# Handing out other work between the four tiles of an image's first attention chunk

## The chip, the core and the metric

The kernel runs on one core of a Trainium2 chip. The metric is the device time of one launch in microseconds (us). The time before is the median of three runs. The profile is one further execution, with the profiler on.

## What is computed

Two images of 128 channels and 64 x 64 pixels pass two layers, all in 32-bit floats. Layer 0 is a group norm and a windowed attention (7 x 7 neighbours, 4 heads) with norms and linear maps around it. Layer 1 takes the 4096 pixels of each image as tokens. It has two parts, and the change lies in the first of them:

```python
# layer 0
x = x + conv_attn(group_norm(x))
# layer 1, first part: attention of an image's 4096 tokens over themselves
t = to_tokens(x)
q = layernorm(t)
sim = (q @ q.T) * 128 ** -0.5
sim[diagonal] = -1e9
t = t + softmax(sim) @ q
# layer 1, second part: long convolution with 16 filters, done in the frequency domain,
# and three short lags, with weights picked by log_w + gumbel
t = t + spectral(layernorm(t)) + short_lags(layernorm(t))
out = from_tokens(t)
```

The attention of layer 1 runs over all 4096 tokens of one image: `sim` is 4096 x 4096 for each image and is symmetric, since queries and keys are the same array.

## The kernel before

**Engines and stages.** Below, PE is TensorE, DVE is VectorE, ACT is ScalarE, POOL is GpSimd, and SP is the engine that issues most transfers. In time the kernel has three stages. Layer 0 of both images takes the first 345 us of the profiled execution. Layer 1's attention runs first for image 0 (from 345.8 us), then for image 1 (from 812.7 us). The convolution in the frequency domain starts at 1295.6 us and lasts to the end.

**The attention, `attention(b, fill)`, line 882.** The 32 tiles of 128 tokens of an image are grouped into 8 chunks of 4 tiles. Because `sim` is symmetric only the 36 pairs of chunks `(a, c)` with `c >= a` are computed. `weights(a, c, k)` makes one tile: a matmul over 128 channels into a PSUM bank (L903[...]), for a diagonal pair an addition that masks the diagonal (DVE, L909), the exponential with its row sums (ACT, L911), and for a diagonal pair the part left of the diagonal, which is turned from the tiles made earlier by transposes on PE (L917) and copied by DVE (L918). So in a diagonal pair tile `k` needs the finished exponentials of tiles 0 to `k-1`. `turned` makes the transposed tiles of a pair off the diagonal (PE L927, DVE L930). `onto` adds a tile's product with the tokens to the chunk `a` itself (L941, PSUM tile `own`), and L968 adds those for chunk `c` (PSUM tile `other`).

**The order.** The four tiles of the first pair (0, 0) are made ahead of the loop, one behind the other. In the loop over pairs, each of the four steps of a pair makes one tile of the *following* pair, multiplies one tile of the present pair onto its chunk, and then calls `fill()`.

**`fill()`, lines 1207 to 1229.** It hands out one step of other work: it takes the generator at the head of a list and runs it to its next `yield`. First comes `urgent`, what follows an image's finished chunks; then `steps`, a list given by the caller. A `yield True` ends the turn of that list and gives out nothing more from it. The instructions of a step are written into the program at that place. The order in which they reach an engine's queue is mostly that of the program, but not always: the framework's own ordering puts forward instructions that it expects to be ready. In this stage no order by hand is in force (the `manual_schedule` blocks at L844 and L1379 cover layer 0 and the convolution).

**What image 0's attention hands out.** `steps` begins with `drain()` (L1231): the rest of layer 0, 72 pieces, three to a step. The first four steps are:

| step | pieces | work |
|---|---|---|
| 1 | k.a, k.tt, k.bn | four transposes of `xa` (PE L200), a copy to `tt` (ACT L684), statistics (DVE L691, L693): the last four token tiles of image 0 |
| 2 | t.yr, k.pw, k.z | POOL alone: a maximum (L660), the reciprocal root of those four tiles (L698, L699), their normalised values `tok` (L704) |
| 3 | t.proj, t.pb, t.add | eight matmuls (PE L602), DVE L613, POOL L636 and L638 |
| 4 | t3.bn, k.b, k.cm | DVE L379 and L381, four transposes of the new `tok` (PE L193), a copy to `cm` (ACT L716) |

Behind the drain come `branch_weights` (L1081), `filters` (L1154) and image 1's `tokens` (L204).

**What image 1's attention hands out.** `steps` begins with what image 0 has left over: the remaining steps of `after` for its chunks 6 and 7, then `short_lags`. `after(b, c, part)` (L985) has seven: (1) transposes of `xa` (PE L992) and the weighted sum into `tt` (DVE L997); (2) a layer norm to `z` (DVE L174, L175, L164; POOL L165; DVE L182); (3) nothing, a `yield True`; its next turn transposes `z` (PE L193) and copies it to `zc` (ACT L1009); (4) and (5) four matmuls each (PE L1028), copies to `ub` by ACT and DVE (L1030) and two stores each (SP L1017); (6) eight small matmuls (PE L1038), copies (L1044) and four stores (SP L1046). Behind these come `filter_matrices` (L1137), whose loads go through SP (L1130) and whose mixing runs on DVE (L1133, L1135, L1146 to L1151), and `load_blocks` (SP L1270).

Of the kernel before, what the change touches and what calls it, by code (L numbers as in the profile page):

```python
# [95 lines left out]
def kernel(  # L96
# [761 lines left out]
    with ap_:  # L858
# [6 lines left out]
        def bank():  # L865
            return ps_m.tile([P, 512], F32, tag="bank", name="bank")
# [15 lines left out]
        def attention(b, fill):  # L882
# [15 lines left out]
            def weights(a, c, k, left=()):  # L898

                n = 4 * CHUNKS[a] + k  # L900
                lo = k * P if a == c else 0
                ps = bank()
                nc.tensor.matmul(  # L903
                    ps[:, lo:], lhsT=cm[b][:, n * P : (n + 1) * P],
                    rhs=cm[b][:, CHUNKS[c] * 512 + lo : (CHUNKS[c] + 1) * 512], start=True, stop=True,
                )
                if a == c:
                    ks = slice(k * P, (k + 1) * P)
                    nc.vector.tensor_tensor(ps[:, ks], ps[:, ks], ndiag, ALU.add)  # L909
                e = ep.tile([P, 512], F32, tag="e", name="e")  # L910
                nc.scalar.activation(  # L911
                    e[:, lo:], ps[:, lo:], AF.Exp, bias=0.0, scale=ASCALE, accum_out=part[:, n, c : c + 1]
                )
                if lo:
                    pt = bank()
                    for j in range(k):
                        nc.tensor.transpose(pt[:, j * P : (j + 1) * P], left[j][:, lo : lo + P], ident)  # L917
                    nc.vector.tensor_tensor_reduce(  # L918
                        e[:, 0:lo], pt[:, 0:lo], one[:, 0:lo], 1.0, 0.0, ALU.mult, ALU.add, part[:, n, 8:9]
                    )  # L920
                return e

            def turned(a, c, m, es):

                pt = bank()
                for k in range(4):
                    nc.tensor.transpose(pt[:, k * P : (k + 1) * P], es[k][:, m * P : (m + 1) * P], ident)  # L927
                et = ep.tile([P, 512], F32, tag="et", name="et", bufs=4)
                n = 4 * CHUNKS[c] + m
                nc.vector.tensor_tensor_reduce(  # L930
                    et, pt, one, 1.0, 0.0, ALU.mult, ALU.add, part[:, n, a : a + 1]
                )
                return et
# [3 lines left out]
            def onto(a, n, e, first, last):  # L937
                nonlocal own
                if first:
                    own = ps_o.tile([P, 512], F32, tag="own", name="own")  # L940
                nc.tensor.matmul(own, lhsT=tok[b][:, n, :], rhs=e, start=first, stop=last)  # L941
                if last:
                    xs = xa[b][:, chunk(a)]
                    if a:
                        nc.vector.tensor_tensor(xs, own, xs, ALU.add)
                    else:
                        nc.vector.tensor_copy(xs, own)
                    fill(CHUNKS[a], part)
# [2 lines left out]
            es = []  # L951
            for k in range(4):
                es.append(weights(0, 0, k, es))
            for i, (a, c) in enumerate(pairs):
                following = pairs[i + 1] if i + 1 < len(pairs) else None
                coming = []
                if a != c:
                    other = ps_o.tile([P, 512], F32, tag="other", name="other")
                for k in range(0, 4, 2):
                    for j in (k, k + 1):  # L960
                        if following:
                            coming.append(weights(*following, j, coming))
                        if a == c:
                            while late:
                                onto(*late.pop(0))
                            onto(a, 4 * CHUNKS[a] + j, es[j], j == 0, a == 7 and j == 3)
                        else:
                            nc.tensor.matmul(  # L968
                                other, lhsT=tok[b][:, 4 * CHUNKS[a] + j, :], rhs=es[j], start=(j == 0), stop=(j == 3)
                            )  # L970
                        if late:
                            onto(*late.pop(0))
                        fill()
                    if a != c:
                        for j in (k, k + 1):
                            late.append((a, 4 * CHUNKS[c] + j, turned(a, c, j, es), False, c == 7 and j == 3))
                if a != c:
                    xs = xa[b][:, chunk(c)]
                    if a:
                        nc.vector.tensor_tensor(xs, other, xs, ALU.add)  # L980
                    else:
                        nc.vector.tensor_copy(xs, other)
                es = coming
# [223 lines left out]
        def filler(b, steps, kept=None):  # L1207

            urgent, done = [], []

            def fill(c=None, part=None):
                if c is not None:
                    done.append(c)
                    urgent.append(after(b, c, part))
                    if len(done) % 4 == 0:
                        held = kept if kept is not None and len(done) == 4 else urgent
                        held.append(short_lags(b, len(done) // 4 - 1))
                    return

                for queue in (urgent, steps):  # L1220
                    while queue:
                        got = next(queue[0], False)
                        if got is None:
                            return
                        if got:
                            break
                        queue.pop(0)

            return fill, urgent
# [17 lines left out]
        steps = [drain(), chosen, filters(), tokens(1, bank)]  # L1247
        fill, left = filler(0, steps)
        attention(0, fill)
        for gen in steps:  # L1250
            for _ in gen:
# [30 lines left out]
        kept = []  # L1282
        fill, left = filler(1, steps, kept)
        attention(1, fill)
        for gen in steps:
            for _ in gen:
# [237 lines left out]
```

## Time and profile before

| | |
|---|---|
| time, median of 3 runs | 2200.89 us (2199.68 to 2202.2) |
| the profiled execution's own time | 2200.82 us |
| its span, first to last instruction | 2199.1 us |
| outside the span | 1.7 us |
| PE busy | 2145.5 us, 98% of the span |
| DVE busy | 952.8 us, 43% |
| ACT busy | 769.9 us, 35% |
| POOL busy | 278.7 us, 13% |
| mean granted TensorE clock | 0.992 |

All times of single instructions below are microseconds from the span's start in this one execution. A profile line of an instruction group reads: start, length, engine, line, operation, output and inputs, count, and in brackets how long the engine had been idle and what released it. The modelled ends of matmuls overlap the next ones, so the cost of a matmul in a stream is read from one start to the next.

### The profile page before, as it was taken

How to read it: one execution, taken by the hardware profiler on the slowest of the kernel's cores; microseconds unless marked ns; L12 is line 12 of the kernel's file. 1: busy time of each engine (PE TensorE's matmuls, PEld its weight loads, DVE VectorE, ACT ScalarE, POOL GpSimd, SP SyncE). 2: the span in 40 equal slices, each digit the busy share in tenths (PEclk: the TensorE clock that was granted, in tenths of full speed). 3: DMA queues.
4: the chain of work that ended last, by engine and by line, in shares of the span. 5: the costliest groups of instructions: out<-in, count | busy, mean ns of one | idle time of the engine just before them, and what ended most of it. 6: DMA issues, size and time to landing. Idle time of an engine off the chain costs nothing.

```text
span 2199.1 us, 32064 instructions
## 1 busy us (share of the span) xinstructions
PE 2145.5 (98%) x12016; PEld 1341.3 (61%) x12016; DVE 952.8 (43%) x3150; ACT 769.9 (35%) x1904; POOL 278.7 (13%) x357
## 2 busy tenths in 40 slices
PE   6999998999999999999999999999999999999998
PEld 4677774545555444544554456767767676767776
DVE  5899985444443356433333543232232323232232
ACT  3889884222332222122223233232232323232232
POOL 3477875200000000000000000000000000000000
PEclk8999999999999999999999999999999999999999
DMA  4222212021000025000001142221221221212101
GB/s 147 62 61 61 62 52 53 0 74 47 25 24 25 23 67 159 24 24 25 1 24 31 44 109 50 50 60 40 60 52 48 50 50 44 56 44 56 40 11 77
DMA packets 170347, 110.56 MB, mean 50 GB/s; under 512 B 21311, under 2 KB 155087, under 8 KB 169680
## 3 DMA queue, kind: packets, MB, share of 16 engines
q1 hardware_dynamic: 169266, 105.01, 17.8%
q8 instruction: 95, 1.56, 0.3%
q0 software_dynamic: 576, 2.10, 0.3%
q10 hardware_dynamic: 350, 1.41, 0.3%
q14 instruction: 60, 0.49, 0.1%
HBM read 73.86 MB, written 34.63 MB: 49 GB/s over the span
## 4 chain that ended last, share of the span: by engine, by line
PE 89%; DVE 5%; POOL 3%; ACT 1%; DMA 1%; issue 1%; SPq 0%; POOLq 0%; DVEq 0%; ACTq 0%
PE acc L1348 25%; PE pc L1336 13%; PE own L941 11%; PE bank L903 10%; PE other L968 8%; PE bank L927 4%; PE bank L333 2%; PE bank L1069 2%; PE bank L543 2%; PE bank L193 2%; PE bank L1028 1%; PE py L1370 1%; PE bank L507 1%; PE po L565 1%; ACT p L530 1%; POOL ln_rs L387 1%
## 5 line engine op out<-in xcount | busy, mean ns | idle before, releaser
L1337 DVE COPY y<-pc 128x512 f32<-128x512 f32 x320 | 221.5, 692 | 351.7 <-PE pc L1336 348.0
L911 ACT ACTIVATE e<-bank 128x512 f32<-128x512 f32 (+3 forms) x288 | 161.6, 561 | 513.9 <-PE bank L903 396.7
L1348 PE MATMUL acc<-y,mpl 128*128 128x256 f32 x1280 | 292.1, 382 | 0.0
L1348 PE MATMUL acc<-y,mmi 128*128 128x256 f32 x1280 | 288.0, 379 | 0.0
L1336 PE MATMUL pc<-ct,ut 64*128 64x512 f32 x1280 | 285.2, 595 | 1.0 <-issue 1.0
L903 PE MATMUL bank<-cm 128*128 128x512 f32 (+3 forms) x576 | 278.4, 565 | 1.4 <-DVE y L654 1.4
L1348 PEld LDWEIGHTS acc<-y,mpl 128*128 128x128 f32 x1280 | 238.1, 190 | 59.4 <-issue 29.6
L1348 PEld LDWEIGHTS acc<-y,mmi 128*128 128x128 f32 x1280 | 242.6, 190 | 32.6
L1337 ACT COPY y<-pc 128x512 f32<-128x512 f32 x320 | 204.5, 639 | 87.0 <-PE pc L1336 86.9
L941 PE MATMUL own<-et,tok 128*128 128x512 f32 x448 | 228.6, 597 | 6.5 <-DVE part L930 6.4
L968 PE MATMUL other<-e,tok 128*128 128x512 f32 x448 | 229.9, 595 | 0.0
L1336 PEld LDWEIGHTS pc<-ct,ut 64*128 64x128 f32 x1280 | 121.5, 187 | 145.9 <-issue 140.7
L930 DVE CUSTOM_DVE_ANT_0 et<-bank,one 128x512 f32<-128x512 f32 x224 | 145.4, 686 | 131.3 <-PE bank L927 131.3
L941 PEld LDWEIGHTS own<-et,tok 128*128 128x128 f32 x448 | 84.4, 191 | 116.9 <-issue 67.1
L1355 ACT COPY ob<-acc 128x256 f32<-128x256 f32 x32 | 19.3, 604 | 387.1 <-PE acc L1348 387.1
L1372 DVE TENSOR_TENSOR xa<-py,xa 128x512 f32<-128x512 f32 x32 | 22.1, 691 | 281.4 <-PE py L1370 281.4
L968 PEld LDWEIGHTS other<-e,tok 128*128 128x128 f32 x448 | 81.9, 191 | 90.1 <-issue 88.5
L927 PEld LDWEIGHTS bank<-ident,e 128*128 128x128 f32 x896 | 102.9, 141 | 55.4 <-issue 50.2
L903 PEld LDWEIGHTS bank<-cm 128*128 128x128 f32 x576 | 94.2, 191 | 65.1 <-issue 41.6
L165 POOL TENSOR_TENSOR ln_rs<-ln_rs,mhalf 128x4 f32<-128x4 f32 x24 | 24.5, 1019 | 811.2 <-DVE ln_rs L164 811.2
L530 ACT ACTIVATE p<-p,mn 128x196 f32<-128x196 f32 x256 | 114.3, 449 | 14.0 <-DVE mn L520 13.5
L927 PE MATMUL bank<-ident,e 128*128 128x128 f32 x896 | 117.2, 274 | 0.0
(215 smaller groups left out, 2342.5 us busy)
## 6 DMA issues: line engine op xcount, KB each, us to landing
ut<-us SPq DMA_DIRECT2D x80, 256.0 KB
us<-ub SPq DMA_DIRECT2D x64, 256.0 KB
vw<-vd SPq DMA_DIRECT2D x256, 49.0 KB
ct<-gs SPq DMA_DIRECT2D x160, 72.0 KB
ct<-gs SPq DMA_DIRECT2D x160, 64.0 KB
gs<-sum SPq DMA_DIRECT2D x20, 256.0 KB
vd<-v SPq DMA_DIRECT2D x128, 32.0 KB
st<-in_m_plus_dram SPq DMA_DIRECT2D x16, 256.0 KB
```

Source lines behind the costliest of these rows:

```text
L193: nc.tensor.transpose(ps[:, j * P : (j + 1) * P], src[:, j, :], ident)
L333: nc.tensor.matmul(pl, lhsT=wg[:, lo : lo + P], rhs=zT, start=True, stop=True)
L530: nc.scalar.activation(p, p, AF.Exp, bias=t[name + "mn"][:, h : h + 1], scale=-1.0, accum_out=t["den"][:, u, h : h + 1],)
L903: nc.tensor.matmul(ps[:, lo:], lhsT=cm[b][:, n * P : (n + 1) * P], rhs=cm[b][:, CHUNKS[c] * 512 + lo : (CHUNKS[c] + 1) * 512], start=True, ...
L911: nc.scalar.activation(e[:, lo:], ps[:, lo:], AF.Exp, bias=0.0, scale=ASCALE, accum_out=part[:, n, c : c + 1])
L927: nc.tensor.transpose(pt[:, k * P : (k + 1) * P], es[k][:, m * P : (m + 1) * P], ident)
L930: nc.vector.tensor_tensor_reduce(et, pt, one, 1.0, 0.0, ALU.mult, ALU.add, part[:, n, a : a + 1])
L941: nc.tensor.matmul(own, lhsT=tok[b][:, n, :], rhs=e, start=first, stop=last)
L968: nc.tensor.matmul(other, lhsT=tok[b][:, 4 * CHUNKS[a] + j, :], rhs=es[j], start=(j == 0), stop=(j == 3))
L1336: nc.tensor.matmul(pc, lhsT=ut[fp, b, par, :], rhs=cv_[fp], start=True, stop=True)
L1337: (nc.scalar.copy if f else nc.vector.tensor_copy)(y[:, 4 * f : 4 * f + 4, :, par, b * 2 * FB + q : (b + 1) * 2 * FB : 2], pc.rearrange("p ...
L1348: nc.tensor.matmul(acc, lhsT=(mmi if l else mpl)[:, k, :], rhs=y[:, 1::2, k, ::-1, :] if l else y[:, 0::2, k, :, :], start=(l == 0 and k = ...
```

## The change

A call of `fill()` is put behind each of the four tiles of an image's first diagonal pair. Each image so hands out four steps between tiles 0, 1, 2 and 3 and ahead of the loop, and every later step moves four places forward. No operation is added or removed: the same steps are handed out in the same order among themselves.

```diff
             es = []
             for k in range(4):
                 es.append(weights(0, 0, k, es))
+                fill()
             for i, (a, c) in enumerate(pairs):
                 following = pairs[i + 1] if i + 1 < len(pairs) else None
                 coming = []
```

## The prediction

> **What bounds the kernel now.** I read the page's busy times and slices first, then PE by stretches, then the chain of waits of PE in the two places that the change touches, then the instructions there in order of time.
>
> ```profile
> PE 2145.5 (98%) x12016; PEld 1341.3 (61%) x12016; DVE 952.8 (43%) x3150; ACT 769.9 (35%) x1904; POOL 278.7 (13%) x357
> ...
> PE   6999998999999999999999999999999999999998
> ...
> PEclk8999999999999999999999999999999999999999
> ```
>
> PE is busy in nearly every slice, so the kernel is bound by PE's work, and the change removes none of it. Only idle PE time, or time at a lower clock, can be won. All of it is 2199.1 - 2145.5 = 53.6 us, most of it in layer 0. The stretches show where the attention has any (columns: length, busy time of PE, weight loads, DVE, ACT, POOL, granted clock, DMA share, GB/s):
>
> ```profile
> 345.83:352.00 6.17, 4.92 (x19) 2.55 (x20) 5.77 (x26) 2.69 (x10) 6.09 (x8) 1.00 0.23 66
> 352.00:360.00 8.00, 7.55 (x30) 4.21 (x29) 3.78 (x21) 1.96 (x5) 7.72 (x9) 1.00 1.03 98
> 812.65:820.00 7.35, 6.31 (x27) 3.02 (x26) 4.82 (x16) 3.60 (x11) 0.00 (x0) 1.00 0.61 154
> 820.00:833.90 13.90, 13.86 (x49) 5.97 (x48) 9.36 (x31) 5.57 (x15) 0.00 (x0) 1.00 0.78 213
> 833.90:837.50 3.60, 0.02 (x1) 0.02 (x1) 2.70 (x12) 0.00 (x0) 1.30 (x1) 0.88 0.70 201
> 837.50:844.50 7.00, 7.00 (x12) 3.10 (x12) 3.81 (x10) 1.79 (x3) 0.00 (x0) 0.57 0.58 167
> 352.00:790.00 438.00, 436.56 (x1563) 220.92 (x1562) 187.93 (x665) 122.59 (x330) 39.14 (x43) 1.00 0.11 30
> 850.00:1240.00 390.00, 388.80 (x1352) 195.35 (x1350) 158.05 (x484) 99.75 (x281) 6.04 (x6) 1.00 0.11 31
> ```
>
> In the middle of image 0 PE lacks 1.4 of 438 us, in that of image 1 1.2 of 390 us. Handing out a step four places earlier there moves it from one full stretch to another and is costed at nothing; the cover is the attention's own matmuls, and if it were gone there would still only be those few waits to gain. What is left are the two starts. For image 1 the waits of PE between 812 and 850 us are three (total, times, longest):
>
> ```profile
> PE own L941 <- DVE part L930: 3.6, 1, 3.6
> PE bank L193 <- DVE z L182: 1.5, 1, 1.5
> PE bank L917 <- ACT e L911: 1.0, 1, 1.0
> ```
>
> In order of time they stand so:
>
> ```profile
> 815.69 0.33 PE L917 MATMUL bank<-ident,e 128*128 128x128 f32 x1 [1.04 <-ACT e L911]
> ...
> 835.71 1.11 DVE L182 TENSOR_SCALAR z<-tt,ln_mv,ln_rs 128x128 f32<-128x128 f32 x4 [0.90 <-POOL ln_rs L165]
> 836.74 0.68 DVE L930 CUSTOM_DVE_ANT_0 et<-bank,one 128x512 f32<-128x512 f32 x1
> ...
> 837.48 2.07 PE L941 MATMUL own<-et,tok 128*128 128x512 f32 x2 [3.62 <-DVE part L930]
> ```
>
> The reader is to see that the big wait isn't in the first pair at all. It is in pair (0, 1): DVE has chunk 7's layer norm (step 2 of `after`, ending with L182) ahead of the turned tile L930, and PE stands still behind that.
>
> [...]L930 stands 5 us behind a norm that it doesn't need. [...]after 3.6 us of idling the clock is 0.57 over the next 7 us, while the idle 1.5 us before 812.49 left it at 1.00.
>
> **The change part by part: image 1.** The first four turns move steps 4, 5 and 6 of `after` for chunk 6 and step 1 for chunk 7 into the gaps between tiles 0 to 3. In the trace these now follow at 818.87, 821.85, 824.82 and 827.23.
>
> *Removed.* (a) The wait of 1.04 us at L917. The cover put before it is step 4: its matmuls take 1.06 us (818.87 to 819.93). So -1.0. (b) The wait of 3.62 us at 837.48: chunk 7's norm now falls into pair (0, 0), which has no turned tile L930, so nothing of that kind queues behind it. So -3.6. (c) The half clock after it: from 837.48 to 843.56 PE did an `own` pair, four transposes, an L903 pair and an `other` pair, which at the full clock take 0.86 + 0.43 + 0.86 + 0.86 = 3.0 us. So 6.1 - 3.0 = -3.1. Sum -7.7.
>
> *Added.* (d) What is late next is `z` of chunk 7 for the transposes L193, now two places after the norm in pair (0, 0). From the end of L992 PE gets there after three L903 pairs and three L941 pairs, 6 x 0.86 = 5.2 us. The norm's chain is seen twice: L992 at 807.80 to the wait's end at 812.49 is 4.2 us from L992's last start, with DVE nearly free; L992 at 827.23 (done about 827.7) to `z` at about 836.1 is 8.4 us, with DVE full of filter mixing and of waits for its loads. The wait is thus 0 to 3.3 us; the norm lands where DVE is busy 9.36 of 13.90 us, so I take 1.5. Behind it on PE wait L903 and L941 of that pair. [...]price 3.1; I take 0.5. (e) Steps 4 to 6 follow each other closer. `ub` has three buffers, and in the trace the copy L1030 at 824.62 on ACT waited for a store to free one (its engine idle 2.84 us). Four stores of steps 4 and 5 and four of step 6 now go out some 6 us earlier on SP, between the filter loads L1130. A copy that waits on ACT holds up the exponentials L911 behind it, and with them L917. Bounds: 0 if the stores land in time, 2.5 us if step 5's copy waits as in the trace; below nothing I see no reason for a gain. I take 0.6. SP's extra 5.5 us of issuing (1.1 + 1.8 + 2.6 at L1017 and L1046) delays filter loads, whose result `mpl` is wanted only at 1309; the price is inside (d), through DVE waiting for loads.
> Image 1: -7.7 + 1.5 + 0.5 + 0.6 = -5.1.
>
> **Image 0.** Steps 1 to 4 of the drain move between its tiles. (f) Of the wait of 1.25 us at L917 (348.82, on ACT e L911) step 1 covers 0.43 (four L200); step 2 has nothing for PE. Step 3's L602, 0.87 us, covers what is left of the idle time behind it. So -0.4, bounds -1.25 and 0. (g) Step 4's transposes L193 need `tok` from POOL. POOL is busy without a break, 6.09 of 6.17 and 7.72 of 8.00 us:
>
> ```profile
> 349.54 1.79 POOL L660 TENSOR_SCALAR y<-y 128x512 f32<-128x512 f32 x1
> 351.31 3.31 POOL L1091 TENSOR_TENSOR sg<-sg,quarter 128x16 f32<-128x16 f32 x1
> 354.60 0.23 POOL L698 TENSOR_SCALAR krs<-kmv 128x4 f32<-128x4 f32 x1
> 354.91 1.04 POOL L699 TENSOR_TENSOR krs<-krs,mhalf 128x4 f32<-128x4 f32 x1
> 356.06 3.51 POOL L704 TENSOR_SCALAR tok<-tt,kmv,krs 128x128 f32<-128x128 f32 x4
> ```
>
> L660 here is a later step's, and L1091 belongs to `branch_weights`: the ordering has put them ahead of step 2 because they were ready sooner. PE would reach step 4 at about 352.2 (tile 3's last L917 at 351.0, plus 0.33 for itself and 0.87 for L602). With the statistics four places earlier (L200 at about 347 instead of 352) POOL could take L698 at 349.5, and `tok` would be whole at about 354.4: a wait of 2.2 us. But instructions that aren't expected to be ready are also moved back (tile 3's last L917 stands behind the next L903 at 350.07), so the likely wait is small: I take +0.5, bounds 0 and 7.4 (next part). The 0.45 us that the same step idles now is kept inside.
> Image 0: -0.4 + 0.5 = +0.1.
>
> **Sum.** -5.1 + 0.1 = -5.0. On the profiled execution: span 2199.1 to 2194.1, own time 2200.82 to 2195.8. It stands 0.07 below the median, so the median of 2200.89 becomes **2195.9 us**. A measurement of this kernel can tell about 0.2%, 4.4 us, from no change; the forecast is just past that.
>
> **Rivals.** *The wait changes its place.* Chunk 7's norm is as slow as at 827.7 to 836.1 and PE waits 3.3 us for `z`, the clock falling by another 3.1. Then only (a) is won with 0.3 of the rest: 2199.6. For it: DVE stood 4.1 and 2.3 us in waits for filter loads between 812 and 850, in front of whatever came behind. Against it: the same norm took 4.2 us at 808.
> *Slower: POOL in image 0.* If POOL keeps its present order, L660 and L1091 ahead of L698, `tok` is whole only at 359.6, as now. PE, in order, stands at L193 from 352.2: 7.4 us, less 0.4 that it idles there now, and 3.1 for the clock; with (f) -0.4 that is +9.7. With image 1's -5.1 it makes 2205.5. For it: POOL's order above is what the trace has. Against it: step 2 gets ready 5 us sooner. The wait turns the balance from about 5 us on, its clock loss counted: that is `tok` whole later than about 355.
> *The change does nothing.* The ordering puts the steps where it had them (it already moves L1133 of `filter_matrices` to 813.12, far ahead of its turn): 2200.9.
>
> **Chances.** The forecast 0.48, of which 0.33 lies over 4.4 us faster, 0.14 within, 0.01 slower; its own range is 2192.5 to 2199. The moved wait 0.25 (0.02, 0.18, 0.05). POOL 0.22 (0.00, 0.03, 0.19), since it may join the moved wait. Nothing 0.05, all within. So faster 0.35, same 0.40, slower 0.25. The range of 8 in 10 reaches from 2191.5, where (d), (e) and (g) are nothing and (f) is whole, to 2206.5, past the POOL case; it leaves out some 0.05 below and 0.12 above.
>
> **What would show it.** Right: L1028 and L1038 stand between the L903 of tiles 0 to 3 of image 1; the wait of L941 on L930 near 837 is gone and with it the half clock; L917 doesn't wait on ACT; L182 precedes L930 of pair (0, 1) by several us. Wrong: a wait of PE L193 on DVE z near 825 of over 3 us; a wait of L917 on ACT behind an L1030 that waits for `ub`; a wait of L193 on POOL tok near 353 of over 3 us; or PE's order as before. The prediction as a whole fails if the middle stretches lose more than 2 us, since it holds them untouched.

## The result, and the profile after

The change makes the kernel slower: 2207.76 us (2204.46 to 2210.65, 11 runs) against 2201.25 us for the kernel before (2198.81 to 2203.62, 11 runs). The ratio is 1.0030, its 95% interval 1.0022 to 1.0038, so the loss is 6.5 us and stands clear of the 0.2% that can be told from no change. The forecast, 2195.9 us, had the wrong sign, and the result lies 1.3 us above the range. The rival that names POOL in image 0 came true. In image 1 the gain was as small as the moved-wait rival had it, but not through the wait that it named.

The profiled execution after took 2207.31 us, with a span of 2205.6 us. In the table a stage of an image runs from its first tile L903 to the next image's, or to the first matmul of the convolution. "Waiting" is the idle time of PE in the stage, without the wait just before the stage's last boundary, which is nearly the same in every kernel (1.5 us in image 0, 1.0 in image 1), and "half clock" the length of the stretches in which the granted clock was one half.

| | before | after | difference |
|---|---|---|---|
| layer 0, up to the first tile of image 0 | 345.83 | 346.68 | +0.85 |
| image 0 | 466.82 | 473.74 | +6.92 |
| – waiting / half clock | 3.8 / 0 | 7.3 / 6.8 | +3.5 / +6.8 |
| image 1 | 482.97 | 481.71 | -1.26 |
| – waiting / half clock | 10.4 / 6.8 | 9.9 / 3.4 | -0.5 / -3.4 |
| convolution to the end | 903.46 | 903.47 | 0.0 |
| span | 2199.08 | 2205.60 | +6.52 |

The 0.85 us lie in code that the change doesn't touch; in the twelve profiled runs of this document layer 0 ends between 344.0 and 350.2 us. The stage of image 0 scatters little: in the four kernels that leave it as it was before it took 466.5 to 466.8 us. The stage of image 1 scatters more: in the three that leave its start as it was (before, and img0 and img0_two below) it took 481.5 to 484.1 us, so the -1.26 us are no more than its scatter. The rest lies in the two starts.

At a granted clock of 0.50 (357.50 to 364.30 us) PE's work takes twice as long: two tiles L903 (two instructions each) from 359.97 us on took 3.41 us, and 1.72 where the clock is 1.00. PE stood for 1.0 of image 0's 6.8 us at half clock and worked for 5.8, so they cost some 2.9. With 3.5 us of waiting that is 6.4 of the 6.9 us that the stage grew by. The other 0.5 are busy time; as an estimate it is the three waits more than before (10 against 7), since a pair that a wait follows is shown as 1.02 us long and one in a stream costs 0.86.

The page after, same rows as before (busy times, then tenths by slice):

```profile
PE 2147.8 (97%) x12016; PEld 1343.0 (61%) x12016; DVE 953.3 (43%) x3150; ACT 769.1 (35%) x1904; POOL 277.9 (13%) x357
...
PE   6899998999999999999999999999999999999998
...
PEclk8999998999999999999999999999999999999999
```

The number of matmuls and of instructions on the other engines is unchanged. One digit of the clock has fallen from 9 to 8, in the seventh slice, 331 to 386 us. It holds image 0's start, but the digit alone would mislead: the slice also has 6.8 us at half clock that belong to layer 0 (from 333.6 us; in the kernel before they came at 314.4, in the slice before). PE in finer stretches of the kernel after (columns as in the prediction's table):

```profile
346.68:353.50 6.82, 5.73 (x28) 3.47 (x28) 6.61 (x33) 2.11 (x7) 6.74 (x8) 1.00 0.21 60
353.50:357.40 3.90, 0.03 (x1) 0.03 (x1) 2.16 (x15) 0.00 (x0) 3.70 (x5) 1.00 0.00 0
357.40:365.40 8.00, 7.02 (x12) 3.06 (x13) 3.06 (x14) 2.99 (x9) 5.02 (x7) 0.57 0.25 22
365.40:800.00 434.60, 434.33 (x1549) 219.15 (x1547) 183.06 (x635) 121.59 (x327) 29.26 (x32) 1.00 0.10 30
...
866.00:868.80 2.80, 0.79 (x3) 0.01 (x1) 2.21 (x6) 0.64 (x2) 0.00 (x0) 1.00 0.40 114
868.80:873.00 4.20, 4.20 (x9) 2.27 (x10) 1.69 (x4) 0.80 (x2) 0.00 (x0) 0.59 0.55 156
873.00:1245.00 372.00, 371.63 (x1290) 187.87 (x1289) 147.66 (x458) 94.50 (x270) 6.04 (x6) 1.00 0.09 25
```

From 353.5 us PE stands for 3.9 us while POOL is busy for 3.7 of them, and then works for 8 us at a mean clock of 0.57. The middle of both images is as full as before (0.3 us idle in 434.6, 0.4 in 372.0): moving steps from one full stretch to another cost nothing, as forecast. What PE waits for at image 0's start, and what POOL does there (timelines of PE and POOL in the kernel after; in brackets the idle time before the instruction and its releaser; lines from 954 on are one higher than before):

```profile
357.37 0.40 PE L193 MATMUL bank<-ident,tok 128*128 128x128 f32 x1 [3.92 <-POOL tok L704]
358.15 0.47 PE L193 MATMUL bank<-ident,tok 128*128 128x128 f32 x1 [0.38 <-POOL tok L704]
```

```profile
350.38 1.80 POOL L660 TENSOR_SCALAR y<-y 128x512 f32<-128x512 f32 x1
352.15 2.92 POOL L1092 TENSOR_TENSOR sg<-sg,quarter 128x16 f32<-128x16 f32 x1
355.06 0.23 POOL L698 TENSOR_SCALAR krs<-kmv 128x4 f32<-128x4 f32 x1
355.37 1.04 POOL L699 TENSOR_TENSOR krs<-krs,mhalf 128x4 f32<-128x4 f32 x1
356.52 3.12 POOL L704 TENSOR_SCALAR tok<-tt,kmv,krs 128x128 f32<-128x128 f32 x4
```

POOL's list is the same as before the change, instruction for instruction, and as close-packed. Only PE comes earlier: it ended its last L917 at about 353.4, and the four tiles of `tok`, one every 0.8 us, end from 357.3 to 359.6. It waits 4.9 us for them in all, where the kernel before waited 0.45. POOL had L1092 ahead of L698, and before that the statistics `kmv` weren't there. DVE makes them (timelines of DVE and ACT after):

```profile
349.59 1.24 DVE L1136 SCALAR_TENSOR_TENSOR mu<-st,wt,mu 128x384 f32<-128x384 f32 x1
350.75 0.86 DVE L691 BATCH_NORM_STATS2 ln_st<-tt 128x6 f32<-128x128 f32 x4
351.54 0.36 DVE L693 BATCH_NORM_AGGREGATE kmv<-ln_st 128x2 f32<-128x6 f32 x4
```

```profile
348.92 0.60 ACT L911 ACTIVATE e<-bank 128x512 f32<-128x512 f32 x1 [5.21 <-DVE wt L1119]
349.51 0.58 ACT L684 COPY tt<-bank 128x512 f32<-128x512 f32 x1
```

The statistics are done at 351.9. They stand behind the last small operations of `branch_weights` and the first mixing of `mu`, which were ready before. Their input was late for the same reason: ACT's copy L684 ends at 350.1, because it stands behind the exponential of tile 0, and that had waited for DVE.

In image 1 the waits of PE after 820.42 us, kernel after (total, times, longest):

```profile
PE bank L193 <- DVE z L182: 5.8, 4, 1.9
PE own L941 <- DVE part L930: 3.9, 5, 2.0
PE own L941 <- DVE xa L945: 0.8, 1, 0.8
PE bank L903 <- DVE ub L1031: 0.4, 1, 0.4
PE bank L917 <- ACT ub L1031: 0.4, 1, 0.4
```

The single wait of 3.6 us of L941 is gone, and with it 6.8 us at half clock. But L941 still waits for 3.9 us in five pieces (5.0 in four before), there are new waits for `z` (0.9 us at 834.93) and for `ub` (twice 0.4), and the longest piece, 2.0 us at 868.79, again has 3.4 us of half clock behind it. In front of that piece stands filter mixing, and DVE waits for its loads (timelines of DVE and PE after, the stretch before 869 us):

```profile
865.37 0.75 DVE L1136 SCALAR_TENSOR_TENSOR mpl<-st,wt,mpl 128x512 f32<-128x512 f32 x1 [1.85 <-DMA st<-in_m_plus_dram]
866.71 0.75 DVE L1136 SCALAR_TENSOR_TENSOR mpl<-st,wt,mpl 128x512 f32<-128x512 f32 x1 [0.59 <-DMA st<-in_m_plus_dram]
...
868.04 0.68 DVE L930 CUSTOM_DVE_ANT_0 et<-bank,one 128x512 f32<-128x512 f32 x1
```

```profile
868.79 1.40 PE L941 MATMUL own<-et,tok 128*128 128x512 f32 x2 [2.02 <-DVE part L930]
```

### The profile page after: what moved, and what is told of

It reads as the page before. It is cut to its first block, busy times and chain, and to the rows that moved or that the text cites. A ratio compares the mean times of both kernels' runs of the same rounds, so it can differ in the third digit from the quotient of the medians.

```text
span 2205.6 us, 32072 instructions
## 1 busy us (share of the span) xinstructions
PE 2147.8 (97%) x12016; PEld 1343.0 (61%) x12016; DVE 953.3 (43%) x3150; ACT 769.1 (35%) x1904; POOL 277.9 (13%) x357
## 4 chain that ended last, share of the span: by engine, by line
PE 88%; DVE 5%; POOL 3%; DMA 2%; ACT 1%; issue 1%; SPq 1%; POOLq 0%; DVEq 0%; ACTq 0%
PE acc L1349 25%; PE pc L1337 13%; PE own L941 11%; PE bank L903 10%; PE other L969 8%; PE bank L927 4%; PE bank L333 2%; PE bank L193 1%; PE bank L1029 1%; PE bank L1070 1%; PE bank L543 1%; PE py L1371 1%; PE bank L507 1%; ACT p L530 1%; PE po L565 1%
## 5 line engine op out<-in xcount | busy, mean ns | idle before, releaser
L903 PE MATMUL bank<-cm 128*128 128x512 f32 (+3 forms) x576 | 280.4, 569 | 1.8 <-DVE y L654 1.4
L941 PE MATMUL own<-et,tok 128*128 128x512 f32 x448 | 228.0, 595 | 4.5 <-DVE part L930 4.4
L930 DVE CUSTOM_DVE_ANT_0 et<-bank,one 128x512 f32<-128x512 f32 x224 | 145.5, 687 | 140.6 <-PE bank L927 140.6
L941 PEld LDWEIGHTS own<-et,tok 128*128 128x128 f32 x448 | 84.2, 190 | 114.3 <-issue 67.0
L903 PEld LDWEIGHTS bank<-cm 128*128 128x128 f32 x576 | 95.3, 192 | 69.5 <-issue 44.9
```

Source lines behind the costliest of these rows:

```text
L903: nc.tensor.matmul(ps[:, lo:], lhsT=cm[b][:, n * P : (n + 1) * P], rhs=cm[b][:, CHUNKS[c] * 512 + lo : (CHUNKS[c] + 1) * 512], start=True, ...
L930: nc.vector.tensor_tensor_reduce(et, pt, one, 1.0, 0.0, ALU.mult, ALU.add, part[:, n, a : a + 1])
```

## The experiments

Ten kernels were run, each beside the kernel before. "Image 0" and "image 1" are the stages of the table, read from each kernel's profiled run; before they take 466.82 and 482.97 us, after the change 473.74 and 481.71. All edits are to the kernel after unless said.

| kernel | median, us | ratio to before, 95% interval | image 0 | waiting / half clock | image 1 | waiting / half clock |
|---|---|---|---|---|---|---|
| img0 | 2209.64 | 1.0031 (1.0019 to 1.0042) | 473.27 | 7.3 / 6.8 | 484.07 | 11.2 / 6.8 |
| img1 | 2200.98 | 0.9994 (0.9986 to 1.0002) | 466.51 | 3.7 / 0 | 483.74 | 11.9 / 3.4 |
| sg_late | 2205.68 | 1.0013 (1.0007 to 1.0020) | 471.84 | 6.4 / 3.4 | 483.12 | 12.8 / 0 |
| pool_order | 2211.06 | 1.0039 (1.0027 to 1.0050) | 475.36 | 8.5 / 6.8 | 482.08 | 11.8 / 0 |
| kb_back | 2207.22 | 1.0022 (1.0014 to 1.0031) | 473.14 | 8.2 / 3.4 | 482.83 | 12.5 / 0 |
| kb_back_sg | 2207.52 | 1.0024 (1.0014 to 1.0033) | 474.54 | 8.5 / 6.8 | 481.22 | 11.0 / 0 |
| kb_back_nopow | 2204.44 | 1.0014 (1.0006 to 1.0023) | 470.19 | 6.6 / 0 | 483.92 | 10.3 / 6.8 |
| img0_two | 2207.68 | 1.0029 (1.0019 to 1.0039) | 472.76 | 6.9 / 3.4 | 481.50 | 10.2 / 3.4 |
| mix_late_before | 2199.51 | 0.9984 (0.9976 to 0.9992) | 466.50 | 3.7 / 0 | 479.46 | 9.3 / 0 |
| img1_mix_late | 2198.21 | 0.9985 (0.9978 to 0.9992) | 466.57 | 3.8 / 0 | 479.10 | 9.0 / 0 |

The kernels before of the different groups lay at 2201.5 to 2202.9 us; the ratios are within a group.

### Each image alone

The turns are given in one image only (img1 has `b == 1` in place of `b == 0`):

```diff
                 es.append(weights(0, 0, k, es))
-                fill()
+                if b == 0:
+                    fill()
```

img0: 

> The four extra turns are given out in image 0 alone. Theory (POOL theory): the whole loss is in image 0, where PE stands at step 4's transposes L193 until POOL has made tok, 4.9 us in four waits, and then runs one window of 6.8 us at half clock. From tile 0 of image 0 to tile 0 of image 1 it should take 6.9 us more than before, and the kernel 6 to 8 us more than before (about 2207 to 2209). Rival (any reordering of this stage costs time, by luck of the order): a part of the loss, more than 2 us, is missing here.

img1: 

> The four extra turns are given out in image 1 alone. POOL theory: nothing of the loss is here; image 1 gains what it gained in the changed kernel, 1.3 us from its tile 0 to the convolution, so the kernel is 0 to 3 us faster than before. Rival (reordering as such): slower than before by 1 us or more.

img0 came out as expected, and so did the time of img1, though its stage image 1 did not gain the 1.3 us. With image 0's turns alone the loss is whole (1.0031), stage image 0 is 6.4 us longer, and the wait at L193 is 4.9 us as with the full change. With image 1's turns alone nothing can be told from no change. Its first 32 tiles were 0.8 us shorter and the rest of the stage 1.5 us longer in the profiled run, where 3.4 us of half clock fell at 1258.9 us after waits of 0.8 and 1.5 us. The kernel before has those two waits too and keeps the full clock there (1.00 from 1240 to 1300 us, where img1 has 0.87 from 1250 to 1262). So the loss of the change is image 0's, and what image 1 gives back is within the scatter.

### Easing POOL

sg_late takes the power of sigma (L1092) out of POOL's list at image 0's start and does it later, in `filter_matrices`, on a copy that is loaded there:

```diff
 # branch_weights
-            nc.sync.dma_start(out=sg, in_=sigma.partition_broadcast(P))
...
-            nc.gpsimd.tensor_tensor(sg, sg, quarter, ALU.pow)
...
 # filter_matrices
+            raw = sp.tile([P, KF], F32, tag="st", name="raw")
+            nc.sync.dma_start(out=raw, in_=sigma.partition_broadcast(P))
...
+            nc.gpsimd.tensor_tensor(sg, raw, quarter, ALU.pow)
```

> The change as it is, but the power of sigma (2.9 us on POOL, standing just ahead of the four tiles' reciprocal root) is computed behind the loads of the filters, so that POOL comes to the four tiles sooner. POOL theory: tok's first tile is ready at about 354.4 instead of 357.4; PE waits 1 us at L193 instead of 3.9, some 1.9 us in all instead of 4.9; no half clock follows; about 6 us faster than the changed kernel, within 1.5 us of before. Rival (the wait is due to the tiles' statistics being late on DVE, not to POOL's queue): the wait stays over 3 us.

Half a hit. POOL starts `tok` right behind L698 and L699, and PE's waits for it fall from 4.9 to 2.4 us. But they don't vanish: each tile of `tok` takes POOL 0.8 us (four in 3.14), and PE wants one every 0.1 (four L193 in 0.44 us at 363.43, where nothing holds them up). The timeline of PE in sg_late:

```profile
354.94 0.33 PE L193 MATMUL bank<-ident,tok 128*128 128x128 f32 x1 [1.02 <-POOL tok L704]
355.72 0.33 PE L193 MATMUL bank<-ident,tok 128*128 128x128 f32 x1 [0.45 <-POOL tok L704]
```

A wait of 1.7 us at L941 (375.2 us) takes the place of part of it, 3.4 us at half clock follow the waits for `tok`, and image 0 is still 5.0 us longer than before.

pool_order keeps POOL's instructions in the order of the program during image 0's attention, so that step 2 stands ahead of what had been put in front of it:

```diff
-        attention(0, fill)
+        with tc.manual_schedule(engines={mybir.EngineType.Pool}):
+            attention(0, fill)
```

> The change as it is, but POOL's instructions in image 0's attention keep the order of the program, so the four tiles' reciprocal root and values stand ahead of the addition t.add, of the later maximum and of sigma's power. POOL theory: the statistics (DVE, done at about 351.9) release POOL at once, PE waits about 1 us at L193, no half clock, 5 to 7 us faster than the changed kernel. If instead POOL's order were harmless, the time stays at that of the changed kernel. A risk on the other side: an in-order POOL that stands before the statistics holds up the later norms, which would show as new waits of PE on DVE z or ACT zT in image 0.

A miss. The wait for `tok` does shrink, to 0.9 us, but the ratio, 1.0039, is the highest here. In POOL's timeline, pool_order:

```profile
353.41 0.23 POOL L698 TENSOR_SCALAR krs<-kmv 128x4 f32<-128x4 f32 x1 [6.76 <-DVE kmv L693]
```

L698, now first, waits 6.8 us for the statistics, and all that stood ahead of it (L636, L638, L660, L1092) waits behind it. PE then waits elsewhere: in image 0 L941 4.5 us for L930 (3.1 at the longest), L333 1.3 for ACT. So the ordering did have a part in making `tok` late: L698 starts 4.1 us after image 0's first L903 here, and 8.4 us after it in the kernel after. But what it had put in front is work that others wait for, and most of it had filled a time in which the statistics weren't there. With `tok` first POOL idles, and the rest comes late in its place.

### Asking for tok later

kb_back keeps all four turns, but the transposes L193 of `tok` and the copy L716 (k.b, k.cm) go from step 4 to step 8, so PE doesn't ask for `tok` before it did:

```diff
+        kb, kcm, eighth = later[10], later[11], later[21]
+        later[10] = later[11] = lambda: None
+        later[21] = lambda: (kb(), kcm(), eighth())
```

> The change as it is, but the two pieces k.b and k.cm (the transposes L193 of tok and their copy) are handed out four steps later, where they stood before the change. Theory 1 (the loss is only that PE stands at these transposes too soon): the wait on tok and the half clock go, 5 to 7 us faster than the changed kernel. Theory 2 (POOL is late for everything behind tok as well): the next transposes, of t3's z, come on PE at about 357.8 and their z at about 361.8, since POOL makes its reciprocal root only after tok (359.9 to 361.0); the wait moves there, about 4 us on DVE or ACT z, and the kernel is at most 2 us faster than the changed one.

kb_back_sg has sg_late's edit as well:

> As kb_back, and the power of sigma computed later as in sg_late, so POOL gets to tok and to t3's reciprocal root 2.9 us sooner. Theory 2: z at about 359.0 against PE at about 357.8, a wait of some 1.3 us and no half clock; from tile 0 of image 0 to tile 0 of image 1 within 2 us of before (466.8 us), the kernel within 2 us of before. If POOL's queue isn't the cause, it stays 4 us or more slower than before.

kb_back_nopow leaves the power out altogether:

> The change with k.b and k.cm back at step 8 and with sigma's power (L1092, 2.9 us of POOL) left out: the part of the computation that is left out is the raising of sigma to 0.25, so the weights sg are wrong by it. kb_back waited 4.0 us for z behind tok; kb_back_sg waited 1.1 for z but 4.1 us at 376.7, where POOL had waited for sigma's load and then did the power in front of the norm's L387. Theory (image 0's start is paced by POOL's queue): with the power gone altogether both waits go; the wait for z is about 1.1 us, none at L944 above 1.5 us, no half clock, and image 0 takes 467.5 to 469.5 us against 466.8 before and 473.7 with the change. Rival (PE wants the results of the drain earlier than the chain of norms through DVE, POOL and ACT can give them, whatever POOL has to do besides): another wait of 2 to 4 us shows up between 360 and 400, and image 0 stays above 471.

In kb_back the wait moves on, nearly whole, to the next thing that POOL feeds (timelines of DVE and PE, kb_back; lines from 843 on are three higher than in the kernel after):

```profile
359.85 0.16 DVE L396 SCALAR_TENSOR_TENSOR ln_nb<-ln_mv,ln_rs 128x4 f32<-128x4 f32 x1 [5.36 <-POOL ln_rs L387]
```

```profile
360.60 1.09 PE L193 MATMUL bank<-ident,z 128*128 128x128 f32 x4 [4.02 <-ACT z L407]
374.85 1.13 PE L944 MATMUL own<-et,tok 128*128 128x512 f32 x2 [1.71 <-DVE part L933]
```

The norm of the next step needs its root from POOL (L387), and POOL does `tok` first. In kb_back_sg the 4.0 us shrink to 1.1, as expected, but 4.1 us appear 16 us later (timelines of POOL and PE, kb_back_sg):

```profile
370.24 2.90 POOL L1143 TENSOR_TENSOR sg<-raw,quarter 128x16 f32<-128x16 f32 x1 [7.32 <-DMA raw<-in_sigma_dram]
373.11 0.23 POOL L386 TENSOR_SCALAR ln_rs<-ln_mv 128x4 f32<-128x4 f32 x1
373.43 1.04 POOL L387 TENSOR_TENSOR ln_rs<-ln_rs,mhalf 128x4 f32<-128x4 f32 x1
```

```profile
376.65 2.07 PE L944 MATMUL own<-et,tok 128*128 128x512 f32 x2 [4.08 <-DVE part L933]
```

POOL had taken the moved power forward again, waited 7.3 us for its load, and the norm stood behind it: the moved work was paid in another place. With the power left out (kb_back_nopow) POOL is free there, and image 0 falls to 470.19 us: no half clock, the wait for `z` 1.1 us as expected, but 2.3 us at L944 where at most 1.5 were expected. Neither theory's range holds this; they share the result. POOL's list, with this one power in it, is about half of the loss: kb_back to kb_back_nopow is 473.14 to 470.19, ten times the scatter of this stage, though in one profiled run of each. The other half, 3.4 us over before, stays with POOL idle (timelines of DVE and PE, kb_back_nopow):

```profile
367.01 0.69 DVE L1169 COPY ph<-pn 128x256 f32<-128x256 f32 x2 [1.33 <-DMA pn<-in_phi_pad_dram]
...
371.57 0.16 DVE L396 SCALAR_TENSOR_TENSOR ln_nb<-ln_mv,ln_rs 128x4 f32<-128x4 f32 x1 [1.76 <-POOL ln_rs L387]
371.65 0.68 DVE L933 CUSTOM_DVE_ANT_0 et<-bank,one 128x512 f32<-128x512 f32 x1
```

```profile
372.40 1.13 PE L944 MATMUL own<-et,tok 128*128 128x512 f32 x2 [2.26 <-DVE part L933]
```

Here the norm's statistics come late on DVE, behind a copy that waits for a transfer; two roots, one behind the other, take POOL 1.3 us each (L386 and L387 from 368.86 to 371.54); DVE stands at L396 for 1.8 us, and L933, which needs nothing of it, stands behind. This is image 1's mechanism at 837 us of the kernel before, now in image 0. In the kernel before these norms came later (L379 at 375.72 us), and the transfers had landed (the copy L1168 at 361.52 waits for none). The transfers themselves are late here (timelines of SP in the kernel before, of DVE and SP in kb_back_nopow):

```profile
351.85 2.54 SPq L1162 DMA_DIRECT2D pn<-in_phi_pad_dram  x2
```

```profile
358.69 0.59 DVE L1136 SCALAR_TENSOR_TENSOR mu<-st,wt,mu 128x384 f32<-128x384 f32 x1
359.30 2.81 SPq L1163 DMA_DIRECT2D pn<-in_phi_pad_dram  x2
```

Before, they were issued 6.0 us after image 0's first L903, here 13.3 us after it. `pn` shares a ring of two buffers, `st`, with the loads of the filter mixing. In kb_back_nopow two mixings of `mu`, which read such buffers, stand in DVE's queue behind norms that wait for POOL, and `pn` is issued as the first of them ends. So the norms moved forward held up loads here too, through the buffers.

### Two turns in place of four

```diff
-                fill()
+                if b == 0 and k < 2:
+                    fill()
```

> Turns in image 0 only, and only after its tiles 0 and 1: steps 1 and 2 lie between the tiles, step 4 two places earlier than before instead of four. PE then reaches step 4's transposes after the second pair of L903 and L941 and eight L602, at about 356.7 on before's clock of time, where tok's first tile comes at about 356.5 to 357.4 and one more every 0.8 us. Theory (PE in order waits for POOL's tok, and only what it comes too early is lost): waits on tok of 1 to 2 us in sum, no half clock, image 0 at 467 to 469 us (+0.2 to +2.2), total 2201 to 2204. Rival (moving any of the steps ahead costs, not the meeting at tok): image 0 at 470 or more, with waits elsewhere.

The wait for `tok` is what the theory said, 2.3 us in sum with none above 1.0, but image 0 is 5.9 us longer and not 0.2 to 2.2. Three items were not in the sum. There is a half-clock stretch of 3.4 us, though no wait is over 1 us: PE was busy 1.4 of 3.7 us while it took `tok` tile by tile (stretches of PE, img0_two):

```profile
353.50:357.20 3.70, 1.39 (x6) 0.61 (x6) 0.00 (x0) 0.07 (x1) 3.54 (x6) 1.00 0.00 0
357.20:360.90 3.70, 3.70 (x6) 1.43 (x6) 1.86 (x10) 1.93 (x5) 2.10 (x3) 0.57 0.00 0
```

There are 0.6 us at L903 for DVE, and two waits of 0.85 us at 404.8 and 420.2 us, where DVE's copy L984 (L982 of the kernel before) stands behind L396, which waits for POOL. So the forward moves cost something at the first meeting with `tok` and again at these two places, where a norm now falls just ahead of an operation that PE needs. The rival's wording ("moving any of the steps ahead costs") is nearer to this than mine.

### Image 1: the mixing held back

mix_late_before is the kernel before with one edit: the filter mixing uses a copy of its weights that DVE can make only when pair (0, 2) of image 1 has written its part to `xa` (L982 at 856.67). The first mixing then starts at 857.6 us in place of 813.1:

```diff
+            wt2 = sp.tile([P, NBR], F32, tag="wt2", name="wt2", bufs=1)
+            late_ = CHUNKS[2] * 512
+            nc.vector.scalar_tensor_tensor(wt2, xa[1][:, late_ : late_ + NBR], 0.0, wt, ALU.mult, ALU.add)
...
-                    mixed(dst[:, k0 : k0 + 4, :], src[:, k0 : k0 + 4])
+                    mixed(dst[:, k0 : k0 + 4, :], src[:, k0 : k0 + 4], wt2)
```

> The kernel before, without the change; the filter mixing on DVE (L1133 to L1151) is held until pair (0, 2) of image 1 is done, by a copy of its weights that reads a value which that pair writes. DVE theory for image 1 (the wait of 3.6 us at 837 comes from DVE's queue being full of the mixing and of its waits for loads): the wait shrinks to under 1.5 us and the half clock goes; image 1 from tile 0 to the convolution takes 476 to 479 us instead of 483, the kernel is 3 to 7 us faster than before. Rival (the norm alone is what blocks L930): the wait stays at about 3 us. Risk: the mixing lands where it is held to and makes new waits of L941 on L930 there.

img1_mix_late is img1 with this edit:

> The four extra turns in image 1 alone, together with the held mixing. If the two gains are of different waits, it is faster than either: the wait of L193 on DVE z near 834 (0.9 us) goes too, image 1 takes 475 to 478 us, the kernel is 4 to 8 us faster than before. If the held mixing has already taken the wait that the turns would take, it equals mix_late_before within 1 us.

With the mixing out of the way the wait of 3.6 us is gone though nothing of the order of chunk 7's norm has changed; no wait of L941 on L930 is above 1.03 us, and image 1 keeps the full clock. The timelines of DVE and PE in mix_late_before, at the place that had 3.6 us:

```profile
835.57 1.11 DVE L182 TENSOR_SCALAR z<-tt,ln_mv,ln_rs 128x128 f32<-128x128 f32 x4 [1.19 <-POOL ln_rs L165]
836.61 0.68 DVE L930 CUSTOM_DVE_ANT_0 et<-bank,one 128x512 f32<-128x512 f32 x1
```

```profile
836.90 1.02 PE L968 MATMUL other<-e,tok 128*128 128x512 f32 x2
837.75 1.02 PE L941 MATMUL own<-et,tok 128*128 128x512 f32 x2
```

The norm still precedes L930, but L930 is in time: PE goes from L968 to L941 without a gap. What made it late before was the mixing and its loads in front of the norm (timeline of DVE before, where the norm starts at 831.6):

```profile
826.83 0.75 DVE L1135 SCALAR_TENSOR_TENSOR mmi<-st,wt,mmi 128x512 f32<-128x512 f32 x1 [2.08 <-DMA st<-in_m_minus_dram]
828.17 0.75 DVE L1135 SCALAR_TENSOR_TENSOR mmi<-st,wt,mmi 128x512 f32<-128x512 f32 x1 [0.59 <-DMA st<-in_m_minus_dram]
```

Both kernels beat the kernel before (0.9984 and 0.9985, 3.3 to 3.5 us) and the changed one. Between the two nothing can be told apart: once the mixing is held back, image 1's early turns bring nothing more that can be told.

## Why the prediction was wrong

**The step that failed is (g)**, the wait at step 4's transposes. I took +0.5 us between bounds of 0 and 7.4. Measured are 4.9 us against 0.45, so +4.4, and behind it 6.8 us at half clock, another 2.9, which stood in the rival's sum but not in the forecast. I had PE at L193 at 352.2, which was right to 0.4 us (353.45, with a start 0.85 later). What was wrong was to let POOL take L698 at 349.5, because the transposes L200 come 5 us sooner. The statistics lie between them, on DVE, and DVE was 6.61 of 6.82 us busy in that stretch. They ended at 351.9, after POOL's L660 had started; and the order still had L1092 next. L698 started at 355.06, which is 4.7 us later than forecast when the later start is taken off. 1.5 of these are the statistics, 0.3 the rest of L660, and 2.9 the power L1092, which I had expected to fall behind step 2. The first part could have been seen in DVE's busy 5.77 of 6.17 us in the table of stretches: I read POOL's share there and not DVE's. The rival had this mechanism at 7.4 us and +9.7 net for image 0; it measured 4.4 and +6.9. It had PE wait until `tok` is whole, but PE transposes each tile as it comes.

The forecast had -5.0 us and the profiled span moved by +6.5. Of the 11.5 us between them image 0 has 6.8, image 1 3.8 and layer 0 0.85.

PE did not pass over the transposes that waited: in the kernel after the next tile's L903 starts at 359.97 us, behind the last L193 (359.70), and in kb_back, where L193 comes later, the same matmul (L906 there) starts at 352.12, right behind tile 3's transposes. So `tok`, asked for early and not ready, stopped the tiles behind it, and with that wait removed the next came up. I priced the step that has the late input and none of those behind it; kb_back shows that the next one stood at nearly the same place, 4.0 us.

**(f)** was -0.4; L917 waits 1.03 in place of 1.25, so -0.2. A wait of 0.8 us of L941 at 366.8, not in my sum, went too. Image 0's waits then are +4.4 - 0.2 - 0.8 = +3.4, and with the clock's 2.9 that is 6.3 of 6.92 us.

**Image 1.** (a) was right: the 1.04 us are gone. (d) was 1.5 and is 0.93; (e) was 0.6 and is 0.85. (b) and (c) were right at their place and wrong as a sum, since L941 waits elsewhere: 3.9 us in place of 5.0, with 3.4 us of half clock (a loss of 1.7) in place of a loss of 3.1. I had put the wait at 837 down to chunk 7's norm, which the turns move. mix_late_before shows that the norm alone doesn't make it: the mixing in front of it does, and the turns move the norm but leave the mixing in DVE's queue. The stage gained 1.26 us against the 5.1 forecast; the moved-wait rival had 1.3. That it is so near is luck: its place was wrong, not `z` but later pairs, and the stage scatters by more than that. Waiting and clock add up to -0.5 - 1.4 = -1.9; the 0.6 us between this and the stage's -1.26 I did not trace.

**What was right.** The middle of both images lost nothing. The order on the engines was the program's, so the change does what it says. And the point from which image 0's wait turns the balance, about 5 us with its clock loss counted, was passed: 4.4 + 2.9.

**What stays open.** The half of image 0's loss that is left without the power (3.4 us) is seen as waits for norms and transfers in one profiled run. Whether it goes when those transfers are early was not tried.

## What to carry to other kernels

Before work is moved into a gap of one engine, follow its input back through every engine that makes it, and read how full each of them is in that stretch, not in the whole span: here, in the 6.82 us after image 0's first L903, PE was busy for 5.73, DVE for 6.61 and POOL for 6.74. Price the step behind the one you move as well: in kb_back, which took the 4.9 us at `tok` away, PE waited 4.0 us for `z`, the next late input. And when a wait stands behind several instructions of another engine, ask which of them made it late: here holding back the filter mixing gained 3.5 us, and moving the norm that stood nearest gained nothing that could be told.

## What was not expected of the hardware

The granted clock fell without any long wait. In img0_two, four waits of 1.0, 0.45, 0.45 and 0.45 us with 0.3 us of matmul between them were followed by 3.4 us at half clock (a mean of 0.57 from 357.2 to 360.9 us), and in sg_late four of the same lengths too (0.57 from 358 to 362). In kb_back_nopow a single wait of 2.3 us left it at full (1.00 from 369 to 375), and in kb_back one of 2.9 us (868.1) did too: from 869.5 us on its pairs start 0.86 us apart. But in the kernel after one of 2.0 us, at 868.8, did not (0.59 from 868.8 to 873.0). Waits of 0.8 and 1.5 us near 1255 were followed by 3.4 us of half clock in img1 (0.87 from 1250 to 1262), while the kernel before has waits of 0.78 and 1.51 us there (at 1254.6 and 1260.2) and a clock of 1.00 from 1240 to 1300. So the length of the longest wait doesn't tell these cases apart. The 0.5 us for the clock in (d) was my estimate, from one wait of 3.6 us with half clock behind it and one of 1.5 us without; what decides between the cases was not shown.
